# Four graph layers on one core: early dense products for four more source tiles in the max-pooling layer, a new rule for handing them out, and three smaller moves at that layer's ends

## The chip, the cores and the metric

The kernel runs on one core of a Trainium2 chip. The metric is the device time of one execution in microseconds (us), as the median of several runs. Rows of the profile come from one profiled execution, whose own time is given beside its span below. In the profile PE is TensorE (PEld its weight loads), DVE VectorE, ACT ScalarE, POOL GpSimd and SP SyncE; "L1870" is line 1870 of the kernel before.

## The reference

There are N = 6250 nodes with 256 features, and E = 100000 edges, sorted by target; a node's target number is the square of a uniform number times N, so low targets have far more edges than high ones. Hidden features are 512 wide.

```
h = relu(layernorm(x))
h = h @ W1_self + mean_over_edges(h[src]) @ W1_neigh + b1              # layer 1
hp = relu(h @ W2_pool + b2_pool)                                       # layer 2: max pooling
h = h @ W2_self + max_over_edges(hp[src]) @ W2_neigh + b2              #   (0 where a node has no edge)
h = (sum_over_edges(h[src]) + h) / (deg + 1) @ W3_neigh + b3           # layer 3
h = h @ W4_self + mean_over_edges(h[src]) @ W4_neigh + b4              # layer 4
out = x + h @ W_fc + b_fc
```

## The kernel before

**Tiles.** Nodes are cut into 49 row tiles of 128, edges into T = 782 steps of 128. The lowest target tiles (12 in layer 1, H3 = 23 in layers 3 and 4) hold most of the edges. For these the edges are counted into a dense adjacency matrix, kept in DRAM as `tab_a` in eight-bit numbers, block [target tile d, source tile s]; their sums are dense products on TensorE. The rest of the edges of layers 1, 3 and 4 are gathered row by row by GpSimd (`ring<-tab_r` in layer 3, one gather of 128 rows a step) and summed by a product with a one-hot matrix (L571, L574). A maximum can't be a product, so layer 2 gathers all 782 steps.

**Layer 2** (its loop begins at L1855; the stretch of the profile from 647.8 to 1780). Steps are taken in six blocks of `BLOCKS = (52, 100, 220, 180, 130, 100)` steps, the last block first, so that high targets are ready first. At each step GpSimd gathers 128 rows into `X` (L1870), and VectorE (`step`, L1843) takes a running maximum over steps: lane p of a step holds the edges of a run, and a mask says where a run goes on. Every second step SP stores the maxima (`stored`, L1849). Where a block ends, runs that go on in the next lane must be joined: `carry` (L1529) transposes the last row on TensorE (`ptcf`), scans it on VectorE (`cTf`), transposes it back (`pcf`) and stores the repaired row. The scan needs two masks, `keepT` and `contT`, one column set per block, which `chains` (L1476) makes beforehand from the target numbers: per block two transposes on TensorE (`rowsf`, L1481), a copy (`rl`, L1485), two comparisons (L1486, L1488) and two small memsets on VectorE. In the kernel before, `chains` runs to its end ahead of the first step.

Beside the steps the loop advances other work a little at a time, all of it written out into the queues in program order: the products of the weight matrices (`products2`, L1494, with `product` at L278: transposes L286 and products L292), from step 8 to 64; the last columns of the dense matrix (`build_narrow`) to step `EARLY_AT` = 310; block ends; and row tiles.

A **row tile** d is made by `done2` (L1698) once the blocks that hold its edges are done: GpSimd gathers its maxima (L1678), TensorE transposes them and multiplies them and the tile's own row with folded weights (L1717 to L1730), ScalarE splits the result into a high part `hi` of 32 bits and a low part `lo` of 16 bits: `hi` is copied, a product with minus the identity (`minus_r`, L1736) subtracts it in the accumulator, and `lo` is copied from what is left (L1739). Two stores put it into `tab_r` (L1746, L1747). `PACE` says how many tiles are begun by which step (19 by step 318, 37 by 612, 49 by 746). Tile 0 alone needs the last block's own end; it is made by `last_done2` (L1620) after the last step. `last_begun` is the lowest tile that doesn't, tile 1.

**Early products.** Layer 3's dense product needs rows of layer 2, but not all at once: for source tiles `EARLY = (10, 42)` the products with all 23 targets are made in layer 2, from step 320. Whenever four row tiles are ready (`BATCH`), `early_products` (L1791) appends, for each target d: SP loads the four blocks of `tab_a` (`ae`, L1802), ScalarE widens them (`aw`, L1789), TensorE adds four pairs of products into an accumulator `pd` (one f16 product, L632, one of 32 bits, L637, per source tile), and ScalarE keeps the sum in `acc3[d]` (L1774) and lays it back for the next batch (L1782). That is 23 x 32 = 736 pairs. They are handed out by `early.advance` (L1916): after step `at`, 736 x (at - 320) / 432 are to be issued. Rows of the tiles in work lie in `SLOTS`; tiles below `KEPT` = 10 stay in `kept_rows` for layer 3.

**Layer 3** (first gather at 1783.9). A ring of 14 slots takes gathers; for each TensorE makes one pair. Between these the dense products of the sources that are left are spread (`late`, L2089: tiles 0 to 9 from `kept_rows`, 42 to 48 from `zt`), for each of the 23 targets. `stream` loads their blocks (`ac`, issued by ScalarE) and widens them (`af`). `zt`, the rows of tiles 42 to 48 (2.75 MB), is loaded by SP (`resident`, L1998) in one transfer, issued after `kept_stores[-1]`, the last store of tile 0. Both `zt` and the stream's buffers lie in the pool `fz3`, which is closed by `turn_to_4` when layer 4's dense products begin. When a target tile is done, `done3` finishes its row.

Of the kernel before, what the change touches and what calls it, by code (L numbers as in the profile page):

```python
# [34 lines left out]
UP3 = float(2 ** 12)  # L35
ROOM3, SEEN3 = float(2 ** 28), float(2 ** 11)
EARLY = (10, 42)
MADE_AT = 64
EARLY_AT = 310
SLOTS = (10, 14)  # L40
# [50 lines left out]
def fast_path(  # L91
# [1361 lines left out]
    with tc.tile_pool(name="fl2c", bufs=1) as ck, ExitStack() as late:  # L1453
# [166 lines left out]
        def last_done2(d):  # L1620
# [43 lines left out]
                nc.tensor.matmul(pm, hT[:, c, :], un[:, c, :], start=False, stop=(c == KH - 1))  # L1664
            hi, lo = row_parts(d)
            nc.scalar.copy(hi, pm)
            nc.tensor.matmul(pm, minus_r, hi, start=False, stop=True, skip_group_check=True)
            kept_stores.append(nc.sync.dma_start(tab_r[d * P : (d + 1) * P, :FH], hi.bitcast(F32)))
            nc.scalar.copy(lo, pm)
            kept_stores.append(nc.sync.dma_start(tab_r[d * P : (d + 1) * P, FH:], lo.bitcast(F32)))  # L1670
            look_at(d, hi, hT)
            yield
# [25 lines left out]
        def done2(d):  # L1698
# [39 lines left out]
            yield from apart_by(2 if apart else 0)  # L1738
            nc.scalar.copy(lo, pm)  # L1739
            look_at(d, hi, hT)  # L1740
            if EARLY[0] <= d < EARLY[1]:
                ready.append((d, r2))
                if len(ready) == BATCH or d == EARLY[0]:
                    early_products()
            yield from apart_by(8 if apart else 0)
            nc.sync.dma_start(tab_r[d * P : (d + 1) * P, :FH], hi.bitcast(F32))  # L1746
            nc.sync.dma_start(tab_r[d * P : (d + 1) * P, FH:], lo.bitcast(F32))  # L1747
            yield


# [7 lines left out]
                    held_by[d] = last[i]  # L1758
                last[i] = d
        assert all(d >= EARLY[0] for d in held_by.values())  # L1760
        early_all = H3 * (EARLY[1] - EARLY[0])
        ready = []
        early = Hub(look=6)
        early_pool, split_pool = [], []
# [26 lines left out]
        def early_products():  # L1791
            batch = dict(ready)
            ss = sorted(batch)
            ready.clear()
            over.update({s: len(early.work) + H3 * len(ss) for s in ss})
            for d in range(H3):
                got = {}
                loaded.append(got)

                def load(d=d, got=got, i=len(loaded) - 1):  # L1800
                    got[0] = early_pool[0].tile([P, BATCH, P], F8, name="ae", bufs=14)
                    nc.sync.dma_start(got[0][:, : len(ss), :].bitcast(BF16),  # L1802
                                      tab_a[d, :, ss[0] : ss[-1] + 1, :])
                    if i >= 4:
                        widened(loaded[i - 4])

                def rows_at(s, got=got):
                    widened(got)
                    return got[1][:, s - ss[0], :], got[0][:, s - ss[0], :]

                i = len(order3)
                order3.append(d)

                def begin(i=i):
                    lay(i)
# [12 lines left out]


        todo = []  # L1830
        for _ in chains():
            pass
        finding = node_rows(wk, psm, rows_of)
        for _ in range(7):
            next(finding)
# [16 lines left out]
        def paced(at):  # L1852
# [2 lines left out]
                    break  # L1855
            return n0 + (n1 - n0) * (at - a0) / (a1 - a0)

        tiles, begun2, begun_at = [], 0, 0
        ends = []
        now = []  # L1860
        at = 0
        for b in reversed(range(NB)):
# [3 lines left out]
            for s0 in range(0, tb, G2):  # L1866
                X = (xmore if at // G2 % 2 else xpool).tile([P, G2, FH], F32, name="X2")
                for k in range(G2):
# [5 lines left out]
                    row, st = X[:, k, :], same[:, t : t + 1]  # L1874
                    if s0 + G2 >= tb:
                        step(row, X[:, 0, :] if k else run, st, row)
                        if k:
                            stored(b, s0 // 2, X)
                    elif k == 0 and s0:
                        step(run, run, st, row)  # L1880
                    elif k:
# [5 lines left out]
                            step(run, run, st, row)  # L1887
                        stored(b, s0 // 2, X[:, :1, :])
                    at += 1
                    if at > 8:  # L1890
                        next(steps, None)
                        if todo and next(todo[0], 0) == 0:
# [111 lines left out]
    with ExitStack() as on:  # L2004
# [44 lines left out]
        with tc.tile_pool(name="fl3", bufs=2) as wk:  # L2049
# [44 lines left out]
            block = stream(zw, [(d, s0, s1) for d in range(H3) for s0, s1 in late], zw, ahead=1)  # L2094
            todo = []
            work = []
            for d in range(H3):
                work += dense([s for s0, s1 in late for s in range(s0, s1)], lambda s, d=d: block(d, s), lambda s: Z3[s], FH, psd,
                              lambda acc, d=d: todo.append(done3(d, acc)), own=d)
            work += [turn_to_4] + turns[0][1]  # L2100
            sums(wk, psg, tab_r, FH, srcE, keyE, jb, H3, done3, 10, Hub(work), wait=14, todo=todo,
# [683 lines left out]
```

## Time and profile before

| | |
|---|---|
| median of three runs | 2477.61 us (2477.28, 2477.61, 2480.75) |
| the profiled execution | 2482.45 us |
| its span, first to last instruction | 2480.6 us |
| TensorE busy | 2143.6 us, 86% |
| VectorE busy | 1915.2 us, 77% |
| ScalarE busy | 1430.8 us, 58% |
| GpSimd busy | 1739.2 us, 70% |
| moved by DMA | 784.91 MB, 316 GB/s over the span |
| mean granted TensorE clock | 0.939 |
| layer 2, first to last row gather | 647.8 to 1758.7 us |
| layer 3, first gather | 1783.9 us |

The busy shares are means over layers with different limits, so no row of this table says what binds. A stretch is read from its own windows: busy time of each engine there, the idle time of an engine and what ended it, and the cadence of the gathers. The span is what the profile covers; the execution's own time is 1.85 us longer.

### The profile page before, as it was taken

What the parts mean: (1) busy time and instruction counts of PE and PEld (TensorE: products, weight loads), DVE (VectorE), ACT (ScalarE), POOL (GpSimd) and SP (SyncE); (2) the same over time, 40 slices, a digit from 0 to 9 for tenths busy, and PEclk for the clock granted to TensorE, in tenths of its full rate; (3) what the DMA queues carried; (4) which work ended last, traced back from release to release, by engine and by line L of the source; (5) the groups of instructions that cost most, each with busy time, mean ns of one, the idle gap of its engine ahead of it and who ended that gap; (6) DMA issues with size and microseconds to landing.
All of it is one profiled execution on the core that took longest, in us unless ns stands there. A gap on an engine that the chain in (4) does not pass through costs nothing.

```text
span 2480.6 us, 35381 instructions
## 1 busy us (share of the span) xinstructions
PE 2143.6 (86%) x9402; PEld 1239.8 (50%) x9402; DVE 1915.2 (77%) x5404; ACT 1430.8 (58%) x2891; POOL 1739.2 (70%) x2013
## 2 busy tenths in 40 slices
PE   4689999999688477479979995999799998799997
PEld 2356666676444233134434442455344444477776
DVE  7899987785789898978868788786567776477655
ACT  5898878676378898855545663655222222244443
POOL 5477776677566776777767777777477777477776
PEclk9799999999899688689989997999899999999999
DMA  9677777777999999999999999999899999899997
GB/s 314 197 232 240 223 209 213 218 221 242 294 334 317 329 366 349 332 349 363 361 312 358 356 361 365 321 360 348 296 378 405 407 407 407 310 351 335 335 305 237
DMA packets 381103, 784.91 MB, mean 316 GB/s; under 512 B 59374, under 2 KB 175830, under 8 KB 380860
## 3 DMA queue, kind: packets, MB, share of 16 engines
q0 software_dynamic: 135184, 471.64, 56.6%
q1 hardware_dynamic: 178984, 252.38, 28.2%
q10 hardware_dynamic: 66724, 58.54, 7.3%
q8 instruction: 76, 1.25, 0.2%
q14 instruction: 135, 1.11, 0.1%
HBM read 573.21 MB, written 209.94 MB: 316 GB/s over the span
## 4 chain that ended last, share of the span: by engine, by line
PE 37%; DMA 35%; DVE 15%; issue 5%; POOL 4%; ACT 3%; ACTq 0%; POOLq 0%; DVEq 0%; SPq 0%
DMA X<-rows,srcIf 13%; PE pd L632 6%; PE pd L637 6%; PE pd L629 4%; DVE run L1843 4%; DMA rows<-X 3%; DMA xq<-acc 3%; DMA ring<-tab_s,srcE 3%; PE pm_w L292 3%; POOL X L1870 3%; DVE X L1843 3%; PE pm_hp L1278 3%; PE pg L571 2%; PE pg L574 2%; PE pm_hp L1272 2%
## 5 line engine op out<-in xcount | busy, mean ns | idle before, releaser
L1870 POOL DMA_INDIRECT X<-rows,srcIf x782 | 746.5, 955 | 302.5 <-issue 151.5
L1843 DVE SCALAR_TENSOR_TENSOR run<-run,samef,X 128x512 f32<-128x512 f32 x758 | 572.6, 755 | 76.5 <-DMA X<-rows,srcIf 70.7
L549 POOL DMA_INDIRECT ring<-tab_h,srcT x402 | 389.8, 970 | 174.9 <-issue 40.5
L1979 ACT CAST af<-ac 128x768 fp32r<-128x768 fp8e4 (+3 forms) x299 | 217.5, 735 | 352.9 <-PE pd L629 122.4
L549 POOL DMA_INDIRECT ring<-tab_r,srcE x254 | 258.4, 1017 | 99.1 <-issue 39.4
L1843 DVE SCALAR_TENSOR_TENSOR X<-X,samef,run 128x512 f32<-128x512 f32 x379 | 282.2, 745 | 54.7 <-DMA X<-rows,srcIf 22.8
L549 POOL DMA_INDIRECT ring<-tab_s,srcE x254 | 245.3, 966 | 94.8 <-PE pg L569 25.3
L603 DVE SCALAR_TENSOR_TENSOR acc<-pg,M,acc 128x256 f32<-128x256 f32 (+2 forms) x556 | 281.3, 532 | 31.5 <-PE pg L574 21.3
L574 PE MATMUL pg<-ring,hot 128*128 128x256 f32 (+1 forms) x656 | 293.3, 455 | 0.0
L637 PE MATMUL pd<-kept_rows,aw 128*128 128x512 f32 x552 | 277.0, 584 | 0.0
L571 PE MATMUL pg<-ring,hot 128*128 128x259 f16 (+1 forms) x656 | 212.0, 326 | 35.5 <-DMA ring<-tab_h,srcT 14.5
L632 PE MATMUL pd<-kept_rows,ae 128*128 128x512 f16 x552 | 215.0, 390 | 7.0 <-DMA ae<-tab_a 5.3
L1774 ACT COPY acc<-pd 128x512 f32<-128x512 f32 x184 | 107.8, 586 | 181.8 <-PE pd L637 181.5
L637 PE MATMUL pd<-Z1h,af 128*128 128x256 f32 x588 | 194.8, 364 | 0.4 <-ACT af L1306 0.4
L1723 PE MATMUL pm_prf<-unf,hTf 128*128 128x512 f32 x384 | 188.6, 615 | 1.1 <-ACT hTf L1713 1.1
L458 PE MATMUL pb<-hm,hs 128*128 128x196 bf16 x480 | 102.2, 271 | 92.3 <-DVE hm L442 60.2
L545 DVE TENSOR_SCALAR hot<-iota_bf,keyE 128x128 fp32r<-128x128 bf16 x508 | 137.7, 297 | 54.8 <-PE pg L574 28.1
L629 PE MATMUL pd<-zt,af 128*128 128x512 f32 x598 | 165.5, 396 | 2.4 <-ACT af L1979 2.4
L632 PEld LDWEIGHTS <-ae 128*128 128x128 fp8e4 x736 | 71.0, 96 | 186.4 <-issue 171.3
L632 PE MATMUL pd<-Z1l,A 128*128 128x259 f16 x588 | 158.5, 280 | 0.0
L574 PEld LDWEIGHTS pg<-ring,hot 128*128 128x128 f32 x656 | 130.8, 199 | 53.7 <-issue 45.2
L464 ACT ACTIVATE A<-pb 128x392 fp8e4<-128x392 f32 x240 | 116.8, 497 | 60.6 <-PE pb L458 59.7
(439 smaller groups left out, 5122.3 us busy)
## 6 DMA issues: line engine op xcount, KB each, us to landing
rows<-X SPq DMA_DIRECT2D x385, 256.0 KB
rows<-hpf SPq DMA_DIRECT2D x49, 256.0 KB
X<-rows,srcIf POOLq DMA_INDIRECT x782
th<-tab_t SPq DMA_DIRECT2D x48, 256.0 KB
ae<-tab_a SPq DMA_DIRECT2D x184, 64.0 KB
tab_a<-A ACTq DMA_DIRECT2D x15, 784.0 KB
ac<-tab_a ACTq DMA_DIRECT2D x115, 96.0 KB
tab_t<-th SPq DMA_DIRECT2D x37, 256.0 KB
```

The lines of the kernel that those rows point to most:

```text
L545: nc.vector.tensor_scalar(hot[j], iota_b, keyT[:, j - jb : j - jb + 1], None, op0=ALU.is_equal)
L549: nc.gpsimd.indirect_dma_start(out=ring[:, j % deep, :].bitcast(F32), out_offset=None, in_=table, in_offset=bass.IndirectOffsetOnAxis(ap=s ...
L571: nc.tensor.matmul(pg[:, : F + counts], hot[j].bitcast(BF16)[:, 1::2], X.bitcast(F16)[:, 2 * F : 3 * F + counts], start=(k == 0), stop=False)
L574: mm = nc.tensor.matmul(pg[:, :F], hot[j], X[:, :F], start=False, stop=(k == n - 1))
L603: nc.vector.scalar_tensor_tensor(acc[d], half, m, acc[d], op0=ALU.mult, op1=ALU.add)
L629: nc.tensor.matmul(hold[0], a[0], z, start=(s == ss[0]), stop=(s == ss[-1]))
L632: nc.tensor.matmul(hold[0][:, : F + extra], a[1], z[1][:, : F + extra], start=(s == ss[0] and hold[1]), stop=False, **more)
L637: nc.tensor.matmul(hold[0][:, :F], a[0], z[0], start=False, stop=(s == ss[-1]), **more)
L1723: nc.tensor.matmul(pm, hT[:, c, :], un[:, c, :], start=False, stop=(c == KH - 1))
L1843: stepped[:] = [nc.vector.scalar_tensor_tensor(put, held, st, row, op0=ALU.mult, op1=ALU.max)]
L1870: nc.gpsimd.indirect_dma_start(out=X[:, k, :], out_offset=None, in_=tab_p, in_offset=bass.IndirectOffsetOnAxis(ap=srcI[:, t : t + 1], axis=0),
L1979: nc.scalar.copy(wide[i][:, :n, :], got[i][:, :n, :])
```

## The change

Six edits, all in layer 2 and at the head of layer 3:

1. **Four more source tiles.** Tiles 6 to 9 also go into early products, for the first 12 targets only (`EARLY_KEPT = (6, 12)`): 48 pairs more in layer 2, 784 in all. In layer 3 the list `late` becomes one per target: for d < 12 it has tiles 4 and 5 in place of 4 to 9, so layer 3 has 343 dense products in place of 391 (23 x 17).
2. **Another pace.** `early_to(at)` takes the pairs and 17 for each row tile not yet begun at step 320 as one load, spreads it evenly over steps 320 to 750, and subtracts 17 for each row tile that `PACE` has begun by then; what is left is the number of pairs to be issued.
3. **Run ends.** `chains` becomes a generator that is advanced once per step from step 4 on, so its twelve parts are issued with steps 4 to 15 instead of before the first gather.
4. **The last block's last two rows** are stored one by one instead of both together.
5. **Tile 0's low part** is a subtraction on VectorE from the accumulator, in place of a product with `minus_r` and a copy on ScalarE.
6. **The rows of tiles 42 to 48** (`zt`) lie in a pool of their own, `fz3r`, and their load is issued after the low part's store of tile 1 (`last_begun`), in place of the last store of tile 0.

```diff
+EARLY_KEPT = (6, 12)
+TILE_PAIRS = 17
...
             nc.scalar.copy(hi, pm)
-            nc.tensor.matmul(pm, minus_r, hi, start=False, stop=True, skip_group_check=True)
             kept_stores.append(nc.sync.dma_start(tab_r[d * P : (d + 1) * P, :FH], hi.bitcast(F32)))
-            nc.scalar.copy(lo, pm)
+            nc.vector.tensor_sub(lo, pm, hi.bitcast(F32))
...
-            if EARLY[0] <= d < EARLY[1]:
+            if EARLY_KEPT[0] <= d < EARLY[1]:
                 ready.append((d, r2))
-                if len(ready) == BATCH or d == EARLY[0]:
+                if len(ready) == BATCH or d == EARLY_KEPT[0]:
                     early_products()
...
-            nc.sync.dma_start(tab_r[d * P : (d + 1) * P, FH:], lo.bitcast(F32))
+            row_store = nc.sync.dma_start(tab_r[d * P : (d + 1) * P, FH:], lo.bitcast(F32))
+            if d == last_begun:
+                kept_stores.insert(0, row_store)
...
-        early_all = H3 * (EARLY[1] - EARLY[0])
+        early_all = H3 * (EARLY[1] - EARLY[0]) + EARLY_KEPT[1] * (EARLY[0] - EARLY_KEPT[0])
...
-            over.update({s: len(early.work) + H3 * len(ss) for s in ss})
-            for d in range(H3):
+            h = H3 if ss[0] >= EARLY[0] else EARLY_KEPT[1]
+            over.update({s: len(early.work) + h * len(ss) for s in ss})
+            for d in range(h):
...
-        for _ in chains():
-            pass
+        ends_of_runs = chains()
...
+        def early_to(at):
+            a0, a1 = EARLY_AT + 10, T - 32
+            n0 = paced(a0)
+            load = early_all + TILE_PAIRS * (NT - n0)
+            return math.ceil(load * min(1.0, (at - a0) / (a1 - a0)) - TILE_PAIRS * (paced(min(at, PACE[-1][0])) - n0))
...
-                        if k:
+                        if b == 0:
+                            stored(b, s0 // 2 + k, X[:, k : k + 1, :])
+                        elif k:
                             stored(b, s0 // 2, X)
...
                     at += 1
+                    if at > 3:
+                        next(ends_of_runs, None)
...
-                        early.advance(math.ceil(early_all * (at - EARLY_AT - 10)
-                                                / (T - 40 - EARLY_AT)))
+                        early.advance(early_to(at))
...
+        zr = fz3.enter_context(tc.tile_pool(name="fz3r", bufs=1, side="right"))
         zw = fz3.enter_context(tc.tile_pool(name="fz3", bufs=1, side="right"))
...
-            late = ((0, 4), (4, KEPT), (EARLY[1], 45), (45, NT))
+            late = [((0, 4), (4, EARLY_KEPT[0] if d < EARLY_KEPT[1] else KEPT), (EARLY[1], 45),
+                     (45, NT)) for d in range(H3)]
...
-            with tc.issue_after(kept_stores[-1].ins):
+            with tc.issue_after(kept_stores[0].ins):
                 for s0, s1 in ((EARLY[1], NT),):
-                    Z3.update(resident(zw, tab_r, FH, s0, s1))
+                    Z3.update(resident(zr, tab_r, FH, s0, s1))
```

More of the change, by code (lines that the diff above doesn't have):

```diff
@@ L2087, in done3 @@
                 yield 1
-            late = ((0, 4), (4, KEPT), (EARLY[1], 45), (45, NT))
+            late = [((0, 4), (4, EARLY_KEPT[0] if d < EARLY_KEPT[1] else KEPT), (EARLY[1], 45),
+                     (45, NT)) for d in range(H3)]
             Z3 = {s: tuple(v[:, slot[s], :] for v in kept_rows) for s in range(KEPT)}
-            with tc.issue_after(kept_stores[-1].ins):
+            with tc.issue_after(kept_stores[0].ins):
                 for s0, s1 in ((EARLY[1], NT),):
-                    Z3.update(resident(zw, tab_r, FH, s0, s1))
-            block = stream(zw, [(d, s0, s1) for d in range(H3) for s0, s1 in late], zw, ahead=1)
+                    Z3.update(resident(zr, tab_r, FH, s0, s1))
+            block = stream(zw, [(d, s0, s1) for d in range(H3) for s0, s1 in late[d]], zw, ahead=1)
             todo = []
@@ L2097, in fast_path @@
             for d in range(H3):
-                work += dense([s for s0, s1 in late for s in range(s0, s1)], lambda s, d=d: block(d, s), lambda s: Z3[s], FH, psd,
+                work += dense([s for s0, s1 in late[d] for s in range(s0, s1)], lambda s, d=d: block(d, s), lambda s: Z3[s], FH, psd,
                               lambda acc, d=d: todo.append(done3(d, acc)), own=d)
```

## The prediction

> **What bounds the kernel now.** I read the windows first, cut at the joints of the max-pooling layer (its gathers run from 647.8 to 1758.7 us) and of the layer behind it, the third, whose gathers begin at 1783.9. Columns: stretch, us, then busy us (instructions) of PE, PEld, DVE, ACT, POOL, then PE clock, DMA share and GB/s.
>
> ```profile
> 1120.00:1245.00 125.00, 123.04 (x455) 60.13 (x455) 105.52 (x207) 66.96 (x132) 91.53 (x97) 1.00 1.02 362
> ...
> 1270.00:1517.00 247.00, 244.85 (x916) 118.86 (x915) 196.62 (x274) 156.61 (x307) 183.14 (x193) 1.00 1.00 350
> 1517.00:1545.00 28.00, 0.35 (x2) 0.38 (x3) 24.53 (x34) 0.47 (x1) 21.26 (x23) 0.56 1.02 367
> 1545.00:1745.00 200.00, 197.24 (x735) 97.47 (x734) 151.85 (x231) 115.87 (x226) 145.85 (x154) 0.99 0.99 342
> ...
> 1840.00:2060.00 220.00, 216.67 (x927) 98.28 (x926) 167.55 (x379) 57.43 (x104) 169.24 (x163) 0.99 1.03 407
> ```
>
> TensorE looks full nearly everywhere. It is not what the pooling layer waits for, as GpSimd's own rows and the groups by tile show (count, then duration min/median/max in ns, first and last start):
>
> ```profile
> 1785.16 0.95 POOL L549 DMA_INDIRECT ring<-tab_r,srcE  x1 [0.30 <-issue]
> ```
>
> ```profile
> L1870 POOL DMA_INDIRECT X<-rows,srcIf x100: 945/949/954, 1398.0 to 1525.8; - x100
> ```
>
> ```profile
> L549 POOL DMA_INDIRECT ring<-tab_r,srcE x45: 943/949/1478, 1783.9 to 1840.0; - x45
> ```
>
> ```profile
> L549 POOL DMA_INDIRECT ring<-tab_r,srcE x155: 945/949/1647, 1850.0 to 2058.6; - x155
> ```
>
> A gather costs GpSimd 0.95 us and 0.30 before the next, 1.25 in all. In the pooling layer 100 row gathers take 127.8 us, 1.29 each, the difference being gathers of other tiles: there GpSimd issues without a pause, and every gather takes its 0.95. That layer is bound by the count of its gathers. In the third layer the first 45 come at 56.1/44 = 1.275, but the 155 from 1850 on at 208.6/154 = 1.355, and single ones stretch to 1.65 us.
>
> Two things could hold them. TensorE is one:
>
> ```profile
> 1903.41 0.39 PE L632 MATMUL pd<-kept_rows,ac 128*128 128x512 f16 x1
> ...
> 1903.87 0.39 PE L571 MATMUL pg<-ring,hot 128*128 128x512 f16 x1
> ...
> 1904.33 0.39 PE L632 MATMUL pd<-kept_rows,ac 128*128 128x512 f16 x1
> ```
>
> A pair (f16 and f32) starts every 0.46 us, without a gap. A step has one pair of its own, and the dense list of this layer has 23 x 17 products, one joint and 46 of layer 4, 438 items over 254 - 14 - 12 = 228 steps, so 1.92 a step: (1 + 1.92) x 0.46 = 1.34 us. The transfers are the other:
>
> ```profile
> DMA packets 33870, 85.41 MB, mean 407 GB/s; under 512 B 6910, under 2 KB 17534, under 8 KB 33854
> ```
>
> That is the DMA view of 1850 to 2060: 0.551 MB for each of 155 gathers, 1.355 us at 407 GB/s, with a DMA share of 1.03 all the way. **I take the transfers as what binds**: if TensorE alone did, GpSimd would wait for ring slots with gathers of unchanged length. Instead its gathers grow longer, and only where the DMA share is over 1.
>
> **The change part by part.** A pair is 0.46 us throughout.
>
> *The four source tiles.* Tiles 6 to 9 go to the pooling layer for 12 of 23 targets: 48 pairs, 22.1 us of TensorE, leave the third layer. The rows for their transfers and the widening:
>
> ```profile
> ae<-tab_a SPq DMA_DIRECT2D x184, 64.0 KB
> ...
> ac<-tab_a ACTq DMA_DIRECT2D x115, 96.0 KB
> ...
> zt<-tab_r SPq DMA_DIRECT2D x1, 2688.0 KB
> ```
>
> ```profile
> L1789 ACT CAST aw<-ae 128x512 fp32r<-128x512 fp8e4 x184 | 114.3, 622 | 21.5 <-DMA ae<-tab_a 21.4
> ...
> L1774 ACT COPY acc<-pd 128x512 f32<-128x512 f32 x184 | 107.8, 586 | 181.8 <-PE pd L637 181.5
> L1782 ACT COPY pd<-acc 128x512 f32<-128x512 f32 x161 | 95.6, 594 | 0.0
> ```
>
> In the third layer, 390 items over the same 228 steps are 1.71 a step and 1.25 us: TensorE would fall to GpSimd's 1.25. The transfers do not fall with it: 12 pieces of 96 KB become 32 KB, 0.79 MB, 1.9 us at 407 GB/s. The 2.75 MB of the last seven row tiles move out too (below). Up to 1840 the gathers ran at 1.275 against 1.25, so at most 44 x 0.025 = 1.1 us comes back there. I take -3.0 for the layer; the bounds are 0 and -22 (TensorE alone binding, and just above GpSimd's floor).
>
> The Trainium skill ("DMA: Bandwidth & Descriptors", Specifications) gives 435 GB/s as the fabric's ceiling and about 358 GB/s as a core's share of HBM. The 407 of this trace is over the second and under the first. By 435, an estimate, 0.548 MB a step would take 1.26 us and nearly the whole 22 us would come through; I hold to the 407 at which these rows stop growing.
>
> In the pooling layer the 48 pairs need TensorE time, 12 more loads on SP (64 KB each, 0.79 MB over some 700 us) and on ScalarE 12 x (0.62 + 0.59 + 0.59) = 21.6 us, which lies beside 156.61 busy of 247. No row store behind the loads on SP is late, as long as TensorE frees their buffers on time.
>
> *The new pace.* Before, pairs handed out grow as 736 x (step - 320)/432; after, 17 pairs are reserved for each row tile: 1292 x (step - 320)/430 less 17 for each tile begun. Up to the end of the 180-step block (step 410) that is 153 against 175 pairs, up to the end of the 220-step block (630) 528 against 600. So TensorE gets 10 us more by the first and 33 us more by the second, and 24 pairs (11 us) less after it. It has idle time at these two places:
>
> ```profile
> PE pcf L1576 <- DVE cTf L1552: 11.8, 1, 11.8
> ```
>
> ```profile
> PE ptcf L1536 <- DVE X L1843: 27.8, 1, 27.8
> ```
>
> TensorE stands in front of the block's end 11.8 and 27.8 us early (the window 1517 to 1545 above is empty), because the carry's transposes sit ahead in its queue. 39.6 us cover 33. So I cost the extra pairs at nothing; the cover leaves 6.5 us. Without it they come out at the end of the layer, where 9.77 us of idle time (last fence) take the first part: 22.1 - 9.8 = 12.3 us. Bounds 0 and +12.3; taken 0.
>
> *Run ends beside the first steps.* Rows at the layer's start, and of the chain of waits there, at the third layer's first gather and, as shares, from 691 to 780:
>
> ```profile
> 642.18 2.02 DMA rows<-hpf
> ```
>
> ```profile
> 1783.29 0.17 DVE oddI L79
> ```
>
> ```profile
> by line: PE pm_w L292 62.1%; PE pm_b L305 13.0%; ACT wT L289 6.2%; PE pt_w L286 6.1%; PE pb L458 4.4%; ACT many L346 3.4%; ACT usA L299 1.3%; issue 1.0%; ACT hs L447 0.7%; ACT weights L297 0.5%; ACT A L464 0.4%; ACTq L282 0.4%; ACT usB L299
> ```
>
> ```profile
> 647.81 0.95 POOL L1870 DMA_INDIRECT X<-rows,srcIf  x1 [16.24 <-DVE contTf L1488]
> ```
>
> ```profile
> 656.05 0.76 DVE L1843 SCALAR_TENSOR_TENSOR run<-X,samef 128x512 f32<-128x512 f32 x1 [7.92 <-DMA X<-rows,srcIf]
> ```
>
> ```profile
> 648.51 2.05 ACTq L282 DMA_DIRECT2D wl<-in_L_gnn_W_self  x2
> ```
>
> ```profile
> 659.75 6.66 DMA wl<-in_L_gnn_W_self
> ```
>
> ```profile
> 657.31 0.64 PE L1348 MATMUL ps_n<-nr,nr 128*128 128x49 f32 x2 [8.70 <-DVE contTf L1488]
> ...
> 658.56 1.94 PE L286 MATMUL pt_w<-identf,wl 128*128 128x128 f32 x8 [0.20 <-PE ps_n L1349]
> ```
>
> ```profile
> L1485 DVE COPY rl<-rowsf x6: 278/282/292, 644.4 to 657.1; 128x128 f32<-128x128 f32 x6
> ...
> L1488 DVE TENSOR_TENSOR contTf<-rowsf,rl x6: 275/284/285, 645.0 to 658.2; 128x127 bf16<-128x127 f32 x6
> ```
>
> The last rows land at 642.18 + 2.02 = 644.20. The third layer's first gather started 0.45 us after its releaser (1783.46 to 1783.91), so here 644.7 is possible: up to 3.1 us sooner. TensorE stands 8.7 us behind the same work; its weight products could start when the first weights land, about 648.51 + 6.66 = 655.2, 3.4 us before 658.56. Against this, the work of four blocks moves from VectorE's idle time behind its first step: 12 instructions of 0.28 us, issued some 0.2 apart, 2.4 us and the small memsets. They wait for transposes queued on TensorE among the weight products, and the next step waits behind them. Bounds -3.4 and +2.9; I take -2.0, nearer the gain, since the chain of waits runs nearly all on TensorE's weight products from 691 to 780, and these start earlier.
>
> *The layer's end.*
>
> ```profile
> 1765.24 1.08 PE L1536 MATMUL ptcf<-identf,X 128*128 128x128 f32 x4 [9.77 <-DVE X L1843]
> ...
> 1773.04 0.32 SPq L1747 DMA_DIRECT2D tab_r<-kept_rows  x1
> ```
>
> ```profile
> 1779.34 0.63 ACT L1617 ACTIVATE hTf<-kept_rows 128x512 f32<-128x512 f32 x1
> ...
> 1779.96 0.57 ACT L1669 CAST kept_rows<-pm_last 128x512 f16<-128x512 f32 x1
> ...
> 1780.56 0.32 SPq L1670 DMA_DIRECT2D tab_r<-kept_rows  x1
> ...
> 1781.24 0.37 SPq L1998 DMA_DIRECT2D zt<-tab_r  x1
> ```
>
> ```profile
> L2078 DVE TENSOR_TENSOR acc<-acc,pm_own x4: 676/677/687, 2121.4 to 2139.3; 128x512 f32<-128x512 f32 x4
> ```
>
> The low part leaves TensorE and ScalarE for one subtraction on VectorE, 0.68 us by the same shape in L2078, from 1779.34 to about 1780.0: the store goes 0.5 us sooner. Behind it on VectorE wait one-hots not needed before 1791. The last two rows stored singly put the first 0.75 us (one step) ahead of the second and halve the transfer before the last gather: -0.5, at a second issue of 0.32. The 2.75 MB load goes behind the store of 1773.04 instead of at 1781.24, needs 6.8 us at 407 GB/s, and can hold the last store by up to 1 us. Taken -1.0, bounds -1.5 and +1.
>
> **Sum**: -3.0 + 0 - 2.0 - 1.0 = -6.0. The profiled execution took 2482.45 us (span 2480.6 and 1.85 around it), 4.8 above the median 2477.61; it would come to 2476.4, the median to 2471.6.
>
> **Rivals.** *TensorE sets the third layer's pace.* For: pairs without a gap. Against: the stretched gathers. Then -22 instead of -3: 2452.6. *The 48 pairs come late.* TensorE still halts at the block ends (its queue order is written beforehand) and the extra work is pushed to the end of the pooling layer: +12.3 - 6.0, 2483.9, slower. For it: TensorE is busy in 197.24 of the 200 us before the end, and the batch of tiles 6 to 9 is whole only when tile 6 is, whose first store is the sixth from the end of these:
>
> ```profile
> 1704.61 0.46 SPq L1746 DMA_DIRECT2D tab_r<-kept_rows  x1
> ```
>
> All 48 pairs must then go into the 54 us before 1758.7, where the last row tiles are made too. Against: 39.6 us of idle time earlier, which can take the other batches' pairs out of that stretch. It decides if the wait of 27.8 us does not shrink by half or more. *Nothing is gained*: the moved run ends cost on VectorE what they free on GpSimd, and the gathers stay at 1.355: only the end's -1.0, 2476.6.
>
> **How the numbers follow.** Forecast 0.42, TensorE's pace 0.15, late pairs 0.25, nothing gained 0.18. A measurement of this kernel tells about 0.2%, 5 us, from no change: below 2472.7 is faster, above 2482.6 slower. Three quarters of the forecast and all of the first rival are faster: 0.46. Four fifths of the late pairs are slower: 0.20; the rest, 0.34, is the same. The range goes from 2455, where most of TensorE's 22 us show, to 2486, the late pairs with the end's +1 in place of -1; the forecast's own is 2465 to 2477.
>
> **What would show it.** First pooling gather near 645 us and products 3 us sooner; the wait of 27.8 us under 10; gathers of 0.95 us throughout the pooling layer; the third layer's at about 1.34 with 407 GB/s, TensorE now with gaps. If they come at 1.25, the transfers did not bind. If GpSimd waits in the pooling layer behind step 320, or the last early product ends after the last step, the cover failed.

## The result

| kernel | median of 12 runs | lowest to highest |
|---|---|---|
| before | 2481.44 us | 2473.76 to 2483.68 |
| changed | 2487.94 us | 2483.37 to 2493.82 |

The changed kernel takes 1.003 of the time before, 95% interval 1.002 to 1.0041: it is slower, by 6.5 us. The forecast was 6.0 us faster, and the range ended at 2486.

Of the three chips that the experiments ran on, two took 2943 to 2995 us for the kernel before and all others, with a spread of 2%. What is said below in microseconds comes from the third, called the quiet chip, where the kernel before takes 2481 to 2484. The other two, the first (e1 to e8) and the second (e13 to e16), are called disturbed, though what slows them isn't shown, and their runs are named as such.

The profiled execution of the changed kernel took 2493.03 us (span 2491.1), 10.6 more than the one before. The order of the instructions on TensorE, VectorE and GpSimd is the same in both up to 640 us, so the 5 us by which the first layer ends later there (first pooling gather 652.74 against 647.81) are spread between executions; in the eight traces of the table below it lies between 644.5 and 654.8. The rest is read from gathers: GpSimd's groups by tile from step 320 to the last pooling gather, for all of the third layer and for its middle; columns as in the prediction.

```profile
L1879 POOL DMA_INDIRECT X<-rows,srcIf x462: 940/946/1406, 1114.1 to 1763.6; - x154
...
L551 POOL DMA_INDIRECT ring<-tab_r,srcE x254: 940/946/1652, 1795.8 to 2141.4; - x127
...
L551 POOL DMA_INDIRECT ring<-tab_r,srcE x156: 940/946/1622, 1853.2 to 2060.3; - x156
```

The last pooling gather starts at 1763.6 and the first of the third layer at 1795.8: 32.3 us, against 25.2 before (1758.66 to 1783.91). **This alone is 7.0 us, about as much as the medians differ.** The windows of the changed kernel for the stretch from step 320 to the end of the pooling layer, for the middle of the third layer and for all of it, and then the same three of the kernel before:

```profile
1114.00:1764.00 650.00, 619.77 (x2288) 300.27 (x2286) 514.36 (x807) 371.28 (x721) 471.32 (x497) 0.97 0.99 347
1853.00:2060.00 207.00, 196.32 (x820) 91.20 (x818) 157.47 (x358) 51.68 (x100) 155.53 (x155) 0.99 1.03 406
1796.00:2156.00 360.00, 318.05 (x1283) 154.51 (x1283) 244.69 (x559) 83.52 (x156) 253.98 (x254) 0.96 0.99 378
```

```profile
1117.00:1759.00 642.00, 592.20 (x2182) 288.99 (x2181) 513.29 (x802) 349.42 (x684) 472.31 (x497) 0.97 1.00 349
1841.00:2050.00 209.00, 206.81 (x886) 94.09 (x884) 158.82 (x359) 55.08 (x98) 160.71 (x155) 0.99 1.03 407
1784.00:2145.00 361.00, 336.78 (x1404) 161.12 (x1404) 245.60 (x561) 91.12 (x159) 258.27 (x254) 0.97 1.00 388
```

TensorE has 27.6 us more to do from step 320 on and 18.7 less in the third layer. The first stretch is 7 us longer in this execution; the third layer is 1 us shorter, and TensorE's idle time in it grows from 24.2 to 42.0 us.

**What holds the transition.** The longest wait of SP's queue in the changed kernel, its issues there, and ScalarE's row that makes tile 0's high part:

```profile
SPq L1669 <- DMA zt<-tab_r: 12.1, 1, 12.1
```

```profile
1777.14 0.32 SPq L1748 DMA_DIRECT2D tab_r<-kept_rows  x1
...
1777.88 0.37 SPq L2010 DMA_DIRECT2D zt<-tab_r  x1
1790.44 0.32 SPq L1669 DMA_DIRECT2D tab_r<-kept_rows  x1
1790.86 0.38 SPq L1671 DMA_DIRECT2D tab_r<-kept_rows  x1
```

```profile
1782.77 0.59 ACT L1668 CAST kept_rows<-pm_last 128x512 fp32r<-128x512 f32 x1 [5.65 <-PE pm_last L1666]
```

Tile 0's high part is ready at 1783.36, but SP issues its store only at 1790.44, when the 2.75 MB load that was put ahead of it has landed, 12.5 us after its issue. In the trace's records the two transfers report to the same completion semaphore, and SP does not issue the second before the first has counted up. The low part's store stands behind it in SP's order, and the gathers of the third layer need both.

### The profile page after: what moved, and what is told of

It is laid out like the page before. It is cut to its first block, busy times and chain, and to the rows that moved or that the text cites. A ratio compares the mean times of both kernels' runs of the same rounds, so it can differ in the third digit from the quotient of the medians.

```text
span 2491.1 us, 35434 instructions
## 1 busy us (share of the span) xinstructions
PE 2154.9 (87%) x9401; PEld 1254.5 (50%) x9401; DVE 1917.1 (77%) x5405; ACT 1442.8 (58%) x2926; POOL 1730.2 (69%) x2013
## 4 chain that ended last, share of the span: by engine, by line
PE 36%; DMA 35%; DVE 15%; issue 5%; POOL 5%; ACT 3%; ACTq 0%; SPq 0%; DVEq 0%; POOLq 0%
DMA X<-rows,srcIf 14%; PE pd L631 6%; PE pd L634 5%; PE pd L639 5%; DVE run L1846 4%; DMA rows<-X 4%; DMA xq<-acc 3%; DVE X L1846 3%; POOL X L1879 3%; DMA ring<-tab_r,srcE 3%; PE pm_hp L1280 3%; PE pm_w L294 3%; PE pm_hp L1274 2%; PE pg L573 2%; PE pg L576 2%
## 5 line engine op out<-in xcount | busy, mean ns | idle before, releaser
L1991 ACT CAST af<-ac 128x640 fp32r<-128x640 fp8e4 (+4 forms) x299 | 211.6, 717 | 366.0 <-PE pd L631 119.1
L639 PE MATMUL pd<-kept_rows,aw 128*128 128x512 f32 x600 | 299.4, 584 | 0.0
L634 PE MATMUL pd<-kept_rows,ae 128*128 128x512 f16 x600 | 234.6, 391 | 12.7 <-DMA ae<-tab_a 7.9
L1777 ACT COPY acc<-pd 128x512 f32<-128x512 f32 x196 | 115.0, 587 | 201.1 <-PE pd L639 200.9
L631 PE MATMUL pd<-z,af 128*128 128x512 f32 x529 | 148.3, 400 | 5.9 <-ACT af L1991 4.6
```

The costliest lines, as they stand in the source:

```text
L631: nc.tensor.matmul(hold[0], a[0], z, start=(s == ss[0]), stop=(s == ss[-1]))
L634: nc.tensor.matmul(hold[0][:, : F + extra], a[1], z[1][:, : F + extra], start=(s == ss[0] and hold[1]), stop=False, **more)
L639: nc.tensor.matmul(hold[0][:, :F], a[0], z[0], start=False, stop=(s == ss[-1]), **more)
L1991: nc.scalar.copy(wide[i][:, :n, :], got[i][:, :n, :])
```

## The experiments

The theory after reading the two traces: the load in front of tile 0's stores costs 7 to 9 us. The rival, from the prediction: the 48 pairs come late in the pooling layer. The stages on the quiet chip, from the starts of the gathers of one profiled execution each (us; the last four rows carry the early tiles; the last column has that execution's time and the kernel's median):

| kernel | first gather to step 320 | 320 to last gather | to layer 3's first | from there to layer 4's first | execution (median) |
|---|---|---|---|---|---|
| before | 468.7 | 642.1 | 25.2 | 361.3 | 2482.5 (2481.4) |
| run ends alone (e12) | 459.4 | 641.9 | 25.8 | 355.3 | 2469.5 (2478.6) |
| run ends and small edits (e10) | 462.2 | 646.1 | 24.2 | 357.8 | 2473.2 (2476.1) |
| the same and the pace (e17) | 464.8 | 644.2 | 24.1 | 359.4 | 2474.5 (2480.8) |
| early tiles and pace alone (e11) | 466.3 | 645.7 | 26.4 | 359.5 | 2485.4 (2485.6) |
| changed, load put back (e9) | 462.9 | 646.6 | 23.3 | 360.2 | 2481.6 (2487.2) |
| changed | 461.4 | 649.4 | 32.3 | 360.3 | 2493.0 (2487.9) |
| changed, again (c1) | 466.8 | 651.4 | 31.5 | 360.0 | 2502.7 (2488.2) |

The same kernel (the last two rows) differs by 5.4 us in the first column and by 2.0 in the second from one execution to the next, and the third layer, which e12 does not touch, is 6.0 us shorter there than before. Some executions also lie well off their kernel's median. So single cells say little, and only the transition column stands clear of this spread: 31.5 and 32.3 with the moved load, 23.3 to 26.4 in the six rows without it.

**The load put back.** Three runs of one kernel:

```diff
-            with tc.issue_after(kept_stores[0].ins):
+            with tc.issue_after(kept_stores[-1].ins):
```

> The changed kernel with one line as before: the 2.75 MB load of tiles 42 to 48 is issued after the last store of tile 0 again (it keeps its own pool). Theory (the load ahead of tile 0's stores is the loss: SP's store of tile 0's high part waits 12.1 us until that load has landed, and the first gather of layer 3 waits for the store): from the last row gather to layer 3's first gather 24 to 26 us in place of 32.3, time 7 us under the changed kernel, about 2481, level with the kernel before or 1 to 2 us under it. Rival (the early pairs are the loss, late at the end of the pooling layer): the time stays within 2 us of the changed kernel, 2486 to 2490.

> The same kernel as e1_zt_last, on another chip (on the first one every stage of every kernel took 18% longer, with a spread of 2% from run to run, in which 7 us can't be told). Theory: 24 to 26 us from the last row gather to layer 3's first gather, time 2479 to 2482 where the kernel before has 2481 and the changed one 2488. Rival (early pairs are the loss): 2486 to 2490.

> The changed kernel with the 2.75 MB load issued after tile 0's last store, once more, for a chip on which the kernel before takes its 2481 us. Theory: 24 to 26 us from the last row gather to layer 3's first gather (32.3 in the changed kernel), the rest as in the changed kernel: pooling layer 1110 to 1112, layer 3 to layer 4's first gather 360 to 361. Rival (early pairs are late): the wait only moves, 30 us or more to the first gather.

On the first chip, where 7 us can't be told, it took 1.0044 of the kernel before (1.0007 to 1.0081) and 1.0047 (1.0019 to 1.0075), with 28.5 and 27.8 us to the first gather of the third layer. On the quiet chip the transition is 23.3 us, 8.9 shorter than in the changed kernel and 1.9 shorter than before: the load is a loss at that place, as the theory said. The whole time does not show the loss. It is 2487.17 us against 2483.24, 1.0011 (0.9991 to 1.0031), where the theory of the second expectation had 2479 to 2482 and its rival 2486 to 2490, so by the time the rival's number came. These are eight runs, with an interval of 5 us either way, and they settle only that the kernel is not shown faster than before with the load put back. SP's issues there:

```profile
1779.51 0.32 SPq L1669 DMA_DIRECT2D tab_r<-kept_rows  x1
1780.24 0.32 SPq L1671 DMA_DIRECT2D tab_r<-kept_rows  x1
1780.66 0.39 SPq L2010 DMA_DIRECT2D zt<-tab_r  x1
```

**The load alone.** The kernel before with edit 6 only, and later the small edits with edit 6 (e14, against e10):

> The kernel before with the move of that load alone (own pool, issued after the low part's store of tile 1). Theory: tile 0's store waits for the load's landing here too, 5 to 8 us from the last row gather to the first gather more, time about 2487. Rival (early pairs are the loss): within 2 us of the kernel before. A third outcome would be that the stores take another completion semaphore than the load, since the whole order is written anew: then it is level as well, and the trace shows the store not waiting for the load.

> e10_ends_only with the load of tiles 42 to 48 moved ahead of tile 0's stores (own pool, after the low part's store of tile 1), and nothing else. Theory: transition from the last row gather to layer 3's first 31 to 33 us in place of 24.2, either because the store of tile 0's high part waits for the load's landing, or because its bytes queue behind the load's; time 7 to 9 us over e10_ends_only, 2483 to 2485 where the kernel before has 2481.7. Rival (the loss in the changed kernel needs the early tiles): within 2 us of e10_ends_only.

Both ran on the disturbed chips: 1.0019 (0.9982 to 1.0056) and 1.0033 (1.0007 to 1.0058) of the kernel before. The transition took 40.7 us in e2, where the seven other executions on that chip took 26.5 to 36.6, and 41.9 in e14, where three others took 36.6 to 38.1. In e14 the store again waits for the load (issued 2197.64; store 2208.51). In e2 the third outcome came: the store has another semaphore and is issued while the load runs, and still the first gather comes 7.4 us after the low part's store, where it is 2.7 to 4.4 elsewhere. Its rows, SP and GpSimd:

```profile
2175.74 0.39 SPq L2000 DMA_DIRECT2D zt<-tab_r  x1
2181.35 0.32 SPq L1668 DMA_DIRECT2D tab_r<-kept_rows  x1
2182.57 0.32 SPq L1670 DMA_DIRECT2D tab_r<-kept_rows  x1
```

```profile
2189.97 0.94 POOL L549 DMA_INDIRECT ring<-tab_r,srcE  x1 [19.86 <-DMA ac<-tab_a]
```

So one way in which the load holds tile 0's rows is shown, the shared semaphore (the changed kernel in both traces, and e14). A second, bytes that go ahead of theirs, is suggested by e2 alone, in the longest of that kernel's twelve executions on a disturbed chip, and stays open. The times of both kernels tell nothing here, since 7 us can't be told on these chips.

**The early tiles and the pace alone** (edits 1 and 2 on the kernel before; `EARLY_KEPT`, `late` per target and `early_to` as in the diff above):

> The kernel before with the four more source tiles and the new pace alone. Theory (their cover in the pooling layer holds; layer 3's transfers bind): pooling layer within 2 us of before from its first gather to its last, layer 3 from first gather to layer 4's first gather 1 to 3 us shorter; time 0 to 4 us under the kernel before. Rival (late pairs): pooling layer 5 us or more longer between step 320 and the last step, time 3 us or more over the kernel before.

> The same kernel as e3_early_alone. Theory (cover holds, layer 3's transfers bind): pooling layer from first to last gather within 2 us of the 1110.9 of before, layer 3 from its first gather to layer 4's first 1 to 3 us under 361.3, time 0 to 4 us under the kernel before. Rival (late pairs): pooling layer 5 us or more longer.

> The kernel before with the four more source tiles and the new pace alone, on a quiet chip. Theory: to step 320 as before (468 to 469), 320 to 630 longer by 4 to 5 us (427 to 428), 630 to the last gather 219 to 221, transition 25, layer 3 360; time 3 to 5 us over the kernel before. Rival (cover holds, the 5 us of 320 to 630 come from the run ends): 423 and time 0 to 2 us under before.

On the first chip 1.0015 (0.9983 to 1.0046) and 1.0032 (1.0002 to 1.0062). On the quiet one 2485.64 against 2481.68, 1.0013 (1.0001 to 1.0026): 4.0 us slower. TensorE's busy time in this kernel (windows for the same three stretches), then its waits from 1100 to 1770 in this kernel and in the one before (us in total, times, longest):

```profile
1117.00:1763.00 646.00, 616.70 (x2288) 299.16 (x2286) 515.01 (x806) 370.93 (x720) 469.90 (x497) 0.98 0.99 349
1846.00:2055.00 209.00, 199.19 (x825) 92.21 (x825) 158.70 (x365) 52.74 (x101) 159.56 (x157) 0.99 1.03 405
1789.00:2149.00 360.00, 321.23 (x1302) 156.27 (x1301) 244.05 (x562) 85.66 (x159) 256.07 (x255) 0.97 1.01 386
```

```profile
PE pcf L1578 <- DVE cTf L1554: 21.3, 2, 12.4
...
PE ptcf L1538 <- DVE X L1846: 6.8, 1, 6.8
```

```profile
PE ptcf L1536 <- DVE X L1843: 39.5, 3, 27.8
PE pcf L1576 <- DVE cTf L1552: 14.5, 2, 11.8
```

Before, TensorE stood idle for 49.8 us of the 642; here for 29.3 of 646. It did 24.5 us more, 20.5 of it went into idle time, and 4 into the length. Before, the waits at the two block ends and at the layer's end sum to 54.0 us (39.5 and 14.5), 9.8 of them at the layer's end and 30.6 at the second block end (27.8 and 2.8). Here 28.1 are left: 12.4 and 8.9 at the block ends, where TensorE waits inside `carry` for VectorE's scan, and 6.8 at the end. The time and the stretch from 630 to the last gather (219.2) are within the last theory, which by then said that the tiles cost; the stretch 320 to 630 (426.5 us) is half a microsecond under it. The traces alone would not carry the 4 us: e10, without the tiles, takes 646.1 from step 320 too. Over the table the stretch is 641.9 to 646.1 without the tiles and 645.7 to 651.4 with them.

**The run ends alone** (edit 3):

> The kernel before with the run ends beside the first steps alone. Theory from the two traces (changed kernel: first gather 3.4 us after the last rows land against 3.6 before, but 461.4 us from first gather to step 320 against 468.7): first gather not sooner, the stretch to step 320 5 to 7 us shorter, and some of it, up to all, given back behind step 320 where work that was hidden comes later; time 0 to 7 us under the kernel before. Rival (that gain belongs to another order of the whole program and not to this edit): the stretch to step 320 within 2 us of 468.7.

> The kernel before with the run ends alone, on a quiet chip. Theory: to step 320 461 to 463, then 423, 219, 25.2 and 361.3; time 5 to 7 us under before. Rival (work is only put off): 320 to 630 428, time within 2 us of before.

On the first chip 1.0026 (0.9995 to 1.0056). On the quiet one 2478.58 against 2481.68, 0.9988 (0.9975 to 1.0): 3.1 us faster, with an upper bound that touches no change, and short of the theory's 5 to 7. The stretch to step 320 is 459.4 to 466.8 us in the six executions with this edit and 466.3 and 468.7 in the two without it; behind step 320 nothing is given back (423.3 us to step 630, 423.0 before). On the disturbed chips that stretch is not shorter: 574.6 to 580.6 us in the five executions with the edit, 557.3 to 579.2 in the seven without. So a small gain on the quiet chip is likely, and it isn't shown as a rule.

**The control, and the small edits without tiles, pace and load** (edits 3, 4 and 5 on the kernel before):

> The changed kernel once more, as a control beside the next three. From its first trace: 461 us from the pooling layer's first gather to step 320 (468.7 before), 428 from 320 to 630 (423.0), 221 from 630 to the last (219.1), 32.3 from there to layer 3's first gather (25.2), layer 3 360.3 (361.3); time 0.2 to 0.4% over the kernel before. If these stage figures belong to one execution and not to the kernel, they come out otherwise by 2 us or more.

> The kernel before with the run ends beside the first steps, the last rows stored singly and tile 0's low part by subtraction; without the early tiles, the pace and the moved load. Theory (run ends give the stretch to step 320, the two small edits give the 1.9 us that the transition with the load put back has over before, the pace and the tiles take the 4 to 5 us between 320 and 630): to step 320 461 to 463, 320 to 630 423, transition 23.3, layer 3 361.3; time 6 to 9 us under the kernel before. Rival (what is won ahead of step 320 is given back behind it whatever the pace): 320 to 630 428, time 0 to 3 us under before.

The control again takes 1.003 (1.0015 to 1.0045) of the kernel before, 2488.25 against 2481.68, with 31.5 us in the transition. Its stretch to step 320 is 5.4 us longer than in the first trace, so that one belongs to the single execution; the other columns repeat within 2.0. The small edits alone take **2476.05 us, 0.9983 (0.997 to 0.9997): faster than both kernels.** The time is just short of the theory's 6 to 9, 5.6 us under the kernel before; the stretch from 320 to 630, 427.8 us, is the rival's in this execution, and 630 to the last gather 218.2. No edit of e10 that e12 (423.3) lacks is in that stretch, so these 4.5 us can't be put down to an edit there. Its gathers, step 320 to the last and then the third layer's:

```profile
L1868 POOL DMA_INDIRECT X<-rows,srcIf x462: 942/949/1475, 1107.2 to 1753.3; - x154
...
L549 POOL DMA_INDIRECT ring<-tab_r,srcE x254: 942/949/1610, 1777.5 to 2118.8; - x127
```

**The pace without the tiles** (e10 with `early_to` in place of the old rule, 736 pairs):

> e10_ends_only with the new pace added, without the four more tiles (736 pairs, spread over one load of pairs and row tiles). Theory (of TensorE's waits at the block ends some 10 to 13 us each can't be filled, the rest, 15 us at step 630, can): TensorE's wait at step 630 shrinks from 25 to about 10 us, its idle time from step 320 to the end of the pooling layer from 46 to about 30 us, so the stretch from 320 to the last gather may get shorter, by up to the 16 us freed, as far as TensorE and not GpSimd sets it: 2 to 4 us under e10's 646; time 0 to 4 us under e10_ends_only. Rival (the pace itself costs: pairs pushed forward make the row tiles late): 2 us or more longer than e10.

> The same kernel as e13_ends_pace, whose first run fell on a chip where every kernel takes 2980. On a quiet chip, theory: TensorE's idle time from step 320 to the last gather 28 to 32 us (46 without the new pace), that stretch 2 to 4 us under the 646 of e10_ends_only; time 2472 to 2476 where the kernel before has 2481.7. Rival (the pace itself costs): the stretch 648 or more, time 2478 or more.

On a disturbed chip 1.0014 (0.9986 to 1.0042), on the quiet one 2480.79 against 2483.49, 0.9991 (0.9975 to 1.0007). The time is in the rival's range, the stretch from step 320, 644.2 us, in neither (between e10's 646.1 and the 641.9 of e12), and TensorE's idle time stays at 47 us, where the theory had 28 to 32. The window, and TensorE's waits from 1100 to 1770:

```profile
1107.00:1752.00 645.00, 597.95 (x2185) 291.74 (x2183) 514.44 (x809) 350.10 (x688) 471.99 (x497) 0.96 1.00 349
```

```profile
PE ptcf L1538 <- DVE X L1843: 25.0, 2, 13.5
PE pcf L1578 <- DVE cTf L1554: 23.9, 2, 12.6
```

Less the 13.5 us at the layer's end and the 12.6 at the first block end, 22.8 are left at the second, against 25.3 in e10: the new pace alone takes little of that wait, and changes the length by less than can be told. That the loss of the early tiles is that of the 48 pairs is therefore the likelier reading; it isn't shown, since no run has the pairs without the new pace, and the two medians (e17 and e10 against the kernel before beside them) leave room for 3 us of the pace's own.

**What binds the third layer.** In one kernel 66 of its 391 pairs are left out (in `dense`, tiles 1 to 3 unless the tile is the target's own), in the other each of its block loads is done twice:

```diff
+            if s in skip and s != own:
+                return
```

```diff
+            if deep == 4:
+                t = pool.tile([P, 7, P], F8, name="ac_twice", bufs=deep + 1)[:, : s1 - s0, :]
+                nc.scalar.dma_start(t.bitcast(BF16), tab_a[d, :, s0:s1, :])
```

> The kernel before; in layer 3 the dense products of source tiles 1, 2 and 3 are left out (66 of 391 pairs, 30 us of TensorE), with all their transfers and the widening kept. If the transfers set layer 3's pace: gathers 45 to 200 stay at 1.34 to 1.36 us each, layer 3 to layer 4's first gather within 3 us of 361.3. If TensorE does: down to GpSimd's 1.25 each, 20 to 26 us shorter.

> The kernel before; in layer 3 the dense products of source tiles 1, 2 and 3 are left out (66 of 391 pairs, 30 us of TensorE), all transfers and the widening kept; on a quiet chip. If the transfers set the pace: gathers 45 to 200 at 1.33 to 1.35 us each, at 405 to 407 GB/s, TensorE's idle time 25 to 30 us more, layer 3 within 3 us of 361. If TensorE does: 1.25 to 1.27 each, 15 us or more shorter.

> The kernel before; every load of a dense block in layer 3 is done twice, the second time into a tile nobody reads (6.4 MB more, 16 us at 407 GB/s; 92 more issues of 0.4 us on ScalarE, which is busy a quarter of the time). If the transfers set the pace: layer 3 12 to 18 us longer, gathers 45 to 200 at 1.41 each. If TensorE does: within 4 us of 361.3.

> The kernel before; every load of a dense block in layer 3 is done twice, the second time into a tile nobody reads (6.4 MB more, 16 us at 407 GB/s); on a quiet chip. If the transfers set the pace: layer 3 12 to 18 us longer, gathers 45 to 200 at 1.40 us each, still at 405 to 407 GB/s. If TensorE does: within 4 us of 361.

All four are single executions on disturbed chips, so they are compared with the kernels beside them. Without the 66 pairs the layer takes 383.4 us where the kernels on that chip with all pairs (e2, e4) take 386.6 and 389.8, and gathers 45 to 200 take 1.470 us each, as theirs do (1.472 and 1.468); on the other chip 390.7 where e13 and e14 take 391.1 and 390.6. With doubled loads it takes 400.9, 12.7 over the mean of e2 and e4, and 403.9, 13.0 over that of e13 and e14. Thirty microseconds of TensorE's work are worth nothing or 5; 6.4 MB cost 13. The rate does not rise with the bytes: over gathers 45 to 200 it is 372 and 370 GB/s with the doubled loads, 370 to 374 in the four kernels beside them. On the quiet chip the comparison of the kernels with and without the early tiles says the same: gathers 45 to 200 take 1.336 to 1.359 us each with the tiles, where TensorE has 22 us less to do, and 1.330 to 1.349 without them.

## Why the prediction was wrong

By the medians of the quiet chip, taken side by side, the changed kernel is 6.6 us over the kernel before (c1) and edits 3, 4 and 5 alone are 5.6 under it (e10). So the early tiles, the pace and the moved load together cost 12.2 us, where the prediction had a gain for the tiles and next to nothing for the load. How the 12.2 divide is less sure. Going by e11 the tiles and the pace cost 4.0, which leaves 8.2 for the load, as the transitions have it (31.5 and 32.3 less 23.3, 8.2 to 8.9). Going by e9, the same kernel with the load put back, the load is worth 2.6 and the tiles and the pace 9.6. Each rests on medians with intervals of 3 to 5 us either way. The gain of 5.6 divides into -3.1 for the run ends (e12) and -2.5 for the two small edits at the end (e10 less e12).

- **The load: the failed step whose cause the traces show.** "The 2.75 MB load ... needs 6.8 us at 407 GB/s, and can hold the last store by up to 1 us" was taken together with the end's gain as -1.0, bounds -1.5 and +1. The load took 12.5 us to land and held the store by 7.1 us (5.3 in c1); the rest of the 8 to 9 us lies behind the low part's store, from which the first gather takes 5.0 and 4.7 us where it takes 2.6 in e9. Only the bandwidth was counted: what waits behind the load on SP, which the step should have asked for, are the two stores that the whole next layer waits for. The small edits' part of the same step had the right sign, and for the subtraction the right size: the low part's store follows the high part's by 0.73 us (1779.51 to 1780.24 above) where it followed by 1.23, the 0.5 us that were taken. The transitions are 24.2, 24.1 and 23.3 us with the small edits, 25.2, 25.8 and 26.4 without them. The -2.5 by the medians has an interval wider than itself.
- **The 48 pairs: the other failed step.** "39.6 us cover 33. So I cost the extra pairs at nothing; the cover leaves 6.5 us." They cost 4 us with their pace by e11, and more by e9. TensorE's two waits at the block ends were counted whole, but a part of each stays in all four kernels with the tiles: 12.4 to 13.2 us at the first (11.8 before), so that nothing went in there, and 9 to 11 at the second (30.6 before). Together some 21 us took work, not 39.6. The rival "late pairs" named the right direction and the wrong place: the last pair was issued 16 us before the last gather, and in e11 the layer is longer between steps 320 and 630 (426.5 against 423.0), not behind them. What makes it longer there isn't shown beyond TensorE's being full between the waits. So the first paragraph's "That layer is bound by the count of its gathers" is too strong: 4 us for 24.5 us of TensorE's work is little, but not nothing. (One figure of this step is slightly off: the new rule gives 177 pairs at step 410, not 175, which is 1 us and changes nothing.)
- **The third layer.** "I take the transfers as what binds": right for the layer's middle, by the runs above and because TensorE, with 18.7 us less to do, stands idle 17.8 us longer. The size was still wrong: -3.0 was taken, and with the early tiles the layer takes 359.5 to 360.3 us, without 355.3 to 361.3. Nothing that can be told came through. Of the 3.0, the 1.1 us from the first 45 gathers did not come: they are 1.273 us apart in the changed kernel as in the one before. The 1.9 for the bytes are less than the spread between executions. The rival "TensorE sets the third layer's pace" (-22) fell. With the ceiling cited from the Trainium skill ("DMA: Bandwidth & Descriptors", Specifications), 435 GB/s, the layer would have gone to 1.26 us a gather, an estimate; over gathers 45 to 200 the eight traces have 402 to 408, and the trace decides for the lower figure.
- **The run ends: right in sign, by another way than the prediction's.** "The last rows land at 642.18 + 2.02 = 644.20 ... so here 644.7 is possible: up to 3.1 us sooner." The first gather is not sooner at all. By the semaphore of the last rows' store it starts 3.6 us after they have landed, in the changed kernel (649.13 to 652.74) as in the one before; the 3.4 in the expectation of e4 is misread. The profile put the wait down to `contTf`, but in the changed kernel the gather runs although part of `contTf` follows 9 us later (GpSimd and VectorE; the first row of the next fence is the gather):

```profile
652.74 0.94 POOL L1879 DMA_INDIRECT X<-rows,srcIf  x1 [15.88 <-DMA weights<-in_L_gnn_W_fc]
...
661.96 0.28 DVE L1490 TENSOR_TENSOR contTf<-rowsf,rl 128x127 bf16<-128x127 f32 x1
```

  Nor are the weight products done sooner, which was the other half of the reasoning: the first transpose for them starts 7.5 to 10.3 us after the first gather with this edit and 10.8 and 9.9 without it, but the last product ends 126 to 128 us after the first gather instead of 121 and 119, and the gathers are no further at step 128 (185.9 to 191.9 us against 185.0 and 185.5). So that -3.1 by the medians lies near the -2.0 taken is luck; what brings it isn't settled.

## What to carry to other kernels

Ahead of moving a transfer earlier on a queue, ask what stands behind it there: a large load in front of the last small store can delay everything that reads the store, and here, where the two shared a completion semaphore, by the load's landing and not by its issue. Of the idle time that an engine spends at a chain through another engine, only what lies ahead of the chain is cover; what lies inside it stayed, 9 to 13 us at each block end in the kernels with the tiles. Work taken from an engine in a layer that another resource bounds comes back as idle time, so move it only out of a layer which that engine bounds.

## What was not expected of the hardware

- The first gather of the pooling layer starts 3.28 us after GpSimd's last wait has ended, the same in all eight traces of the table to the hundredth; the first of the third layer starts 0.7 us after its last. What fills the 3.28 us isn't shown.
- The same program takes 19 to 20% longer on two chips. GpSimd's gathers keep their length there, with more time between them, and TensorE's granted clock is 0.88 to 0.89 where the quiet chip has 0.93 to 0.94; what slows them isn't shown. The gathers of the pooling layer on the quiet chip (changed kernel) and on the first one (the same with the load put back); behind the bar stand busy time, mean and the idle time before them:

```profile
L1879 POOL DMA_INDIRECT X<-rows,srcIf x782 | 743.7, 951 | 304.3 <-issue 148.6
```

```profile
L1879 POOL DMA_INDIRECT X<-rows,srcIf x782 | 742.4, 949 | 546.9 <-issue 226.1
```
